# Adding the two state products of every second scan step on GpSimd instead of in TensorE's accumulation

## Chip, core and metric

One core of a Trainium2 chip runs the whole program in one launch. The metric is the device time in microseconds (us), as the median of several runs. One execution was also recorded by the hardware profiler; spans, durations and waits below come from that execution.

## What is computed

Four blocks follow one another on a batch of 8 images of 64 channels and 64 x 64 pixels: an attention and depthwise convolution block, two window-attention blocks with MLPs, a dynamic 3 x 3 filter block, and a state-space block. The change lies in the scan of the last one. For each image and each of four directions k, with 128 channels d and 16 states n, it runs along all 4096 positions:

```python
def step(h, inp):
    u_t, dt_t, B_t, C_t = inp
    h = h * jnp.exp(dt_t[..., None] * A) + dt_t[..., None] * B_t[:, :, None, :] * u_t[..., None]
    return (h, jnp.einsum('bkcn,bkn->bkc', h, C_t))
```

The last line is what matters here: the output y of a position is the sum over the 16 states of h times C.

## The kernel before

**The scan.** Channels lie on the 128 partitions, positions in the free dimension. A unit is one image, one direction and one chunk of TD = 512 positions; it has eight steps of two states each. There are 8 images x 4 directions x 8 chunks x 8 steps = 2048 steps. A step i goes through these places:

- `fetch` (L1670) loads two rows of B or of C from DRAM onto all partitions, a 128x1024 tile, through SP's DMA queue. B and C have three buffers each.
- `products` (L1677) multiplies B by dt x u on GpSimd into a tile `vd` of 128x1024 (L1680). `vd` has six buffers; a buffer is free again when TensorE has read it.
- `step` (L1682): for each of the two states ScalarE computes exp(dt A) into PSUM (L1700), VectorE runs the scan over the 512 positions (L1703), ScalarE copies the last column into `carry` for the next chunk (L1711). Then h is multiplied by C into the same `vd`.
- `sums` (L1719) adds both halves of `vd` into one PSUM tile `yd`, with a matmul by the identity each (L1730). Sixteen such matmuls make one unit's y. At the unit's end VectorE adds `yd` to the image's sum Y (L1739 to L1744).

**Two forms of the product with C.** The variable `rp` (L1689) is 0 in even steps of the images 0 to 5. There GpSimd multiplies both states in one 128x1024 instruction (L1714). In odd steps, and in all steps of the images 6 and 7, GpSimd multiplies the first state (L1716, 128x512) and VectorE the second (L1717).

**What lies beside the scan.** `tile_kernel` runs `front(0)`, the first three blocks and the scan's inputs for the first two images, by itself. Then `scans(p)` runs the scan of the image pair p and, between its steps, pieces of other work: `back(p-1)`, which is the scan's output projection and the closing convolutions of the pair before, and `front(p+1)`. Each piece is a `yield` with a cost; after each scan step, pieces are emitted until their cost keeps pace with the step (L1639). So a given piece of the other work stands beside a given step. The fourth pair has only `back(2)` beside it, and `back(3)` runs alone at the end.

**What sets the order.** A scheduler takes the instructions in about the order in which they were emitted, works out which are ready, and fixes one order for each engine. Each engine then takes its own queue strictly in that order. One order is written out by hand: `behind` (L1731) puts the first sum matmul of step i-1 behind the product with C of step i in the schedule (`st["w"]`), without a wait.

Of the kernel before, what the change touches and what calls it, by code (L numbers as in the profile page):

```python
# [11 lines left out]
ALU = mybir.AluOpType  # L12
# [11 lines left out]
DI, NST, RNK, KDIR = 128, 16, 4, 4  # L24
# [201 lines left out]
class _Net:  # L226
# [353 lines left out]
    def in_range(self, pool):  # L580

        nc, tc = self.nc, self.tc
        m = self.sums.shape[1] * 64
        m2 = m + 2 * 4 * NH
        n = m2 + B * KDIR * NTD
        sums = self.sums.rearrange("p a b c -> p (a b c)")
        ok = pool.tile([P, n], F32, name="ok", tag="ok")
        top = pool.tile([P, n], F32, name="top", tag="top")
        cnt = self.const.tile([P, 1], F32, name="cnt", tag="cnt")
        bad = self.const.tile([1, 1], mybir.dt.int32, name="bad", tag="bad")  # L590
        nc.vector.tensor_scalar(ok[:, 0:m], sums, 1e-28, None, ALU.is_gt)
        nc.vector.tensor_scalar(top[:, 0:m], sums, 1e28, None, ALU.is_lt)
        nc.vector.tensor_tensor(ok[:, 0:m], ok[:, 0:m], top[:, 0:m], ALU.mult)
        for i, test in enumerate((ALU.is_lt, ALU.is_gt)):
            ws = self.wsum[:, i].rearrange("p b c -> p (b c)")
            d = ok[:, m + 4 * NH * i : m + 4 * NH * i + 4 * NH]
            nc.vector.tensor_scalar(d, ws, (1e28, 1e-28)[i], None, test)
        nc.vector.tensor_scalar(
            ok[:, m2:n], self.esum.rearrange("p a b c -> p (a b c)"), 1e28, None, ALU.is_lt
        )  # L600
        nc.vector.tensor_reduce(cnt, ok, AX.X, ALU.add)
        with tc.tile_pool(name="psr", bufs=1, space=PSUM) as ps:
            pc = ps.tile([1, 1], F32, name="pcnt", tag="pcnt")
            nc.tensor.matmul(pc, lhsT=cnt, rhs=self.ones[:, 0:1], start=True, stop=True)
            nc.vector.tensor_scalar(bad, pc, P * n - 0.5, None, ALU.is_lt)
        return nc.values_load(bad[0:1, 0:1], min_val=0, max_val=1, skip_runtime_bounds_check_because="a comparison gives 0 or 1")
# [541 lines left out]
class _Direct:  # L1148
# [82 lines left out]
    def layer0(self, p):  # L1231
# [11 lines left out]
        with tc.tile_pool(name="w0", bufs=2) as wk:  # L1243
# [38 lines left out]

            sums = net.sums[:, p]
            nc.vector.tensor_reduce(sums, parts, AX.X, ALU.add)
            rec = wk.tile([P, 2, 32], F32, name="rec", tag="rec", bufs=1)
            nc.vector.reciprocal(rec, sums)
# [395 lines left out]
    def step(self, i, st):  # L1682

        nc, w, net = self.nc, self.w, self.net
        wk, ps = self.sw, self.ps
        u = self.units[i // 8]
        k, c, at, CC, v = u["k"], u["c"], u["at"], st["C"], st["v"]

        n0, rp = 2 * (i % 8), i % 2 or u["image"] >= B - 2  # L1689
        rev = k >= 2  # L1690

        def along(t):
            return t[:, ::-1] if rev else t

        h = wk.tile([P, 2 - i % 2, TD], F32, name="hd", tag=f"h{i % 2}", bufs=1)
        hs = []
        for j in range(2):
            n = n0 + j
            da = ps.tile([P, TD], F32, name="dad", tag="da")
            nc.scalar.activation(da, u["du"][:, 0], AF.Exp, scale=net.As[:, k, n : n + 1])  # L1700
            first = 0.0 if at == 0 else self.carries[:, n : n + 1]
            to = da if rp and j else h[:, j]
            nc.vector.tensor_tensor_scan(along(to), along(da), along(v[:, j]), first, ALU.mult, ALU.add)  # L1703
            hs.append(to)
            if at < NTD - 1 and (rp or j):
                ends = h[:, :, 0] if rev else h[:, :, TD - 1]
                cs = self.carries[:, n0 : n0 + 2]
                if rp:
                    ends = to[:, 0:1] if rev else to[:, TD - 1 : TD]
                    cs = self.carries[:, n : n + 1]  # L1710
                nc.scalar.activation(cs, ends, AF.Copy)  # L1711

        if rp == 0:
            st["w"] = nc.gpsimd.tensor_tensor(v, h, CC, ALU.mult)  # L1714
        else:
            st["w"] = nc.gpsimd.tensor_tensor(v[:, 0], h[:, 0], CC[:, 0], ALU.mult)  # L1716
            nc.vector.tensor_tensor(v[:, 1], hs[1], CC[:, 1], ALU.mult)  # L1717

    def sums(self, i, st, after=None):  # L1719

        nc, w, net = self.nc, self.w, self.net
        wk, ps = self.sw, self.ps
        u = self.units[i // 8]
        k, c = u["k"], u["c"]
        if i % 8 == 0:
            u["y"] = ps.tile([P, TD], F32, name="yd", tag="y", bufs=1)
        y = u["y"]
        for j in range(2):
            n = 2 * (i % 8) + j
            m = nc.tensor.matmul(y, lhsT=w["ident"], rhs=st["v"][:, j], start=(n == 0), stop=(n == NST - 1))  # L1730
            if after is not None and j == 0:  # L1731
                net.behind(m, after)
        if i % 8 < 7:
            return

        yd = net.part(self.Y, k, c)
        yp = y.rearrange("p (a b) -> p a b", b=64)
        if u["nth"] == 0:
            nc.vector.scalar_tensor_tensor(yd, self.img(u["x"]), net.dsum, yp, ALU.mult, ALU.add)  # L1739
        elif u["nth"] < 3:  # L1740
            nc.vector.tensor_tensor(yd, yd, yp, ALU.add)  # L1741
        else:
            o = wk.tile([P, TD], F32, name="yo", tag="yo", bufs=1)
            nc.vector.tensor_tensor(self.img(o), yd, yp, ALU.add)  # L1744
            nc.sync.dma_start(u["out"][:, c * TD : (c + 1) * TD], o)
# [134 lines left out]
```

## Time and profile before

The median of three runs is 14083.28 us (14071.26 to 14084.42). The profiled execution took 14074.21 us; its span, from the first to the last instruction, is 14072.3 us, at a mean granted TensorE clock of 0.865.

| stage (what stands beside the scan) | us | steps with L1714 | TensorE busy | VectorE busy | GpSimd busy |
|---|---|---|---|---|---|
| front(0) alone, 0 to 1905 | 1905 | 0 | 1597 | 400 | 2 |
| attention, 1905 to 2983 | 1078 | 76 | 993 | 502 | 630 |
| depthwise convolution, to 3179 | 196 | 20 | 137 | 180 | 162 |
| windows and MLP, to 4159 | 980 | 90 | 865 | 721 | 744 |
| layer 2, to 4551 | 392 | 30 | 364 | 239 | 242 |
| scan sources and back, to 5188 | 637 | 58 | 430 | 476 | 482 |
| back, pooling part, to 5433 | 245 | 16 | 161 | 195 | 131 |
| attention, to 6266 | 833 | 52 | 793 | 307 | 421 |
| depthwise convolution, to 6462 | 196 | 17 | 136 | 166 | 151 |
| windows and MLP, to 7393 | 931 | 76 | 826 | 637 | 617 |
| layer 2, to 7736 | 343 | 20 | 320 | 181 | 174 |
| scan sources and back, to 8569 | 833 | 77 | 547 | 610 | 637 |
| back, pooling part, to 8716 | 147 | 10 | 87 | 140 | 75 |
| attention, to 9647 | 931 | 57 | 881 | 348 | 477 |
| depthwise convolution, to 9843 | 196 | 19 | 135 | 181 | 160 |
| windows and MLP, to 10725 | 882 | 72 | 788 | 599 | 580 |
| layer 2, to 11117 | 392 | 25 | 362 | 215 | 205 |
| scan sources and back, to 11690 | 573 | 56 | 368 | 429 | 454 |
| fourth pair and the end, to 14072 | 2382 | 0 | 1548 | 1907 | 1830 |

The limits of the stages are those of the lines that run in them (attention L1258, windows L1420 and L1492, layer 2 L1541). A busy time is the time in which the engine had at least one instruction under way. Instructions that lie across a limit are counted on both sides, so the third column adds up to 771 where there are 768. One L1714 stands for a pair of steps, an even and an odd one: four state products summed by TensorE. In a profile line, the first number after the bar is the busy time of the group in us, the second the mean duration of one in ns; what follows is the idle time of the engine just before, and what ended it. PEld is TensorE's loading of weights, which lies beside the matmuls.

### The profile page before, as it was taken

How to read it: one execution, taken by the hardware profiler on the slowest of the kernel's cores; microseconds unless marked ns; L12 is line 12 of the kernel's file. 1: busy time of each engine (PE TensorE's matmuls, PEld its weight loads, DVE VectorE, ACT ScalarE, POOL GpSimd, SP SyncE). 2: the span in 40 equal slices, each digit the busy share in tenths (PEclk: the TensorE clock that was granted, in tenths of full speed). 3: DMA queues.
4: the chain of work that ended last, by engine and by line, in shares of the span. 5: the costliest groups of instructions: out<-in, count | busy, mean ns of one | idle time of the engine just before them, and what ended most of it. 6: DMA issues, size and time to landing. Idle time of an engine off the chain costs nothing. (4 is left out here: it accounts for less than half of the span.)

```text
span 14072.3 us, 141532 instructions
## 1 busy us (share of the span) xinstructions
PE 11340.1 (81%) x46358; PEld 4189.8 (30%) x46358; DVE 8432.1 (60%) x9763; ACT 7036.3 (50%) x15453; POOL 8173.2 (58%) x4111
## 2 busy tenths in 40 slices
PE   9888879979889668998889666998988866666665
PEld 2244222224433222223433222222443222222221
DVE  0222254467776875347675767336666677998884
ACT  5533145555553645555562644555554454454442
POOL 0000035677776765456674685456666678879991
PEclk9866679989889889998898788999888878988996
DMA  0000034456555764345553675345554577878882
GB/s 17 1 1 1 5 136 153 161 187 211 195 196 181 241 206 156 127 147 181 175 197 133 225 247 180 128 144 175 170 173 168 181 244 256 276 241 291 294 291 70
DMA packets 705498, 2379.22 MB, mean 169 GB/s; under 512 B 81060, under 2 KB 81188, under 8 KB 703980
## 3 DMA queue, kind: packets, MB, share of 16 engines
q1 hardware_dynamic: 681024, 2315.57, 48.5%
q10 hardware_dynamic: 23724, 54.50, 1.0%
q8 instruction: 367, 6.01, 0.2%
q14 instruction: 383, 3.14, 0.1%
HBM read 2269.08 MB, written 100.66 MB: 168 GB/s over the span
## 5 line engine op out<-in xcount | busy, mean ns | idle before, releaser
L1680 POOL TENSOR_TENSOR vd<-B,du 128x1024 f32<-128x1024 f32 x2048 | 4842.5, 2369 | 3955.8 <-DVE xacc L1217 1888.8
L1730 PE MATMUL yd<-vd,pack 128*128 128x512 f32 x8192 | 4577.0, 686 | 1175.1 <-POOL vd L1714 419.8
L1703 DVE TENSOR_TENSOR_SCAN hd<-dad,carry,vd 128x512 f32<-128x512 f32 x2464 | 3092.6, 1270 | 1081.7 <-ACT dad L1700 681.2
L1700 ACT ACTIVATE dad<-du,As 128x512 f32<-128x512 f32 x4096 | 2711.7, 679 | 985.0 <-DVE hd L1703 728.8
L1730 PEld LDWEIGHTS yd<-vd,pack 128*128 128x128 f32 x8192 | 1592.5, 212 | 3853.7 <-issue 1753.0
L1714 POOL TENSOR_TENSOR vd<-hd,C 128x1024 f32<-128x1024 f32 x768 | 1810.9, 2358 | 1365.4 <-DVE hd L1703 694.1
L1716 POOL TENSOR_TENSOR vd<-hd,C 128x512 f32<-128x512 f32 x1280 | 1634.9, 1278 | 271.7 <-DVE hd L1703 244.6
L1272 ACT ACTIVATE e<-s 128x512 f32<-128x512 f32 x2048 | 1199.2, 591 | 1030.0 <-PE s L1266 1028.1
L1703 DVE TENSOR_TENSOR_SCAN dad<-dad,carry,vd 128x512 f32<-128x512 f32 x1120 | 1426.0, 1273 | 62.7 <-ACT dad L1700 62.5
L1266 PE MATMUL s<-X 64*128 64x512 f32 x4096 | 1350.1, 646 | 114.1 <-ACT e L1272 113.8
L1258 PE MATMUL po<-e,VT 128*64 128x512 f32 x4096 | 1145.1, 629 | 17.0 <-ACT e L1272 17.0
L1711 ACT ACTIVATE carry<-hd 128x1 f32<-128x1 f32 (+1 forms) x1792 | 357.1, 201 | 1172.7 <-DVE hd L1703 1161.9
L1717 DVE TENSOR_TENSOR vd<-dad,C 128x512 f32<-128x512 f32 x1280 | 858.7, 671 | 82.1 <-ACT carry L1711 74.8
L1266 PEld LDWEIGHTS s<-X 64*128 64x128 f32 x4096 | 365.3, 186 | 1065.4 <-issue 820.8
L1420 PEld LDWEIGHTS w_av<-vals,w_e 64*64 64x64 f32 x16384 | 612.7, 159 | 178.0 <-ACT w_e L1410 69.9
L1420 PE MATMUL w_av<-vals,w_e 64*64 64x9 f32 x16384 | 638.5, 216 | 23.6 <-ACT w_e L1410 23.5
L1703 DVE TENSOR_TENSOR_SCAN hd<-dad,vd 128x512 f32<-128x512 f32 x352 | 420.2, 1210 | 203.0 <-ACT dad L1700 92.0
L1741 DVE TENSOR_TENSOR Y<-Y,yd 128x512 f32<-128x512 f32 x128 | 124.6, 973 | 656.0 <-PE yd L1730 655.7
L1410 ACT ACTIVATE w_e<-w_e 128x512 f32<-128x512 f32 x512 | 310.4, 627 | 382.2 <-DVE w_e L1405 254.9
L1655 PE MATMUL pdd<-xs,xdt 128*128 128x512 f32 x512 | 323.4, 718 | 204.3 <-DVE hd L1703 96.7
L1711 ACT ACTIVATE carry<-dad 128x1 f32<-128x1 f32 x1120 | 189.9, 170 | 589.1 <-DVE dad L1703 587.0
L1405 DVE TENSOR_TENSOR w_e<-w_s,bias 128x512 f32<-128x512 f32 x512 | 328.5, 682 | 248.4 <-PE w_s L1393 248.1
(247 smaller groups left out, 11078.1 us busy)
## 6 DMA issues: line engine op xcount, KB each, us to landing
B<-rows SPq DMA_DIRECT2D x2048, 512.0 KB, 5.0
C<-rows SPq DMA_DIRECT2D x2048, 512.0 KB, 4.5
xs<-xt SPq DMA_DIRECT2D x128, 256.0 KB, 2.9
xs<-xc SPq DMA_DIRECT2D x128, 256.0 KB, 3.1
xc<-xcv ACTq DMA_DIRECT2D x64, 256.0 KB, 4.3
zs<-z ACTq DMA_DIRECT2D x64, 256.0 KB, 3.9
xt<-XT ACTq DMA_DIRECT2D x32, 512.0 KB, 7.5
rows<-bc SPq DMA_DIRECT2D x256, 64.0 KB, 1.9
```

The source lines that it names most:

```text
L1258: nc.tensor.matmul(po[half[im]], lhsT=VT[:, t, half[im]], rhs=es[im], start=(t == 0), stop=(t == 31))
L1266: nc.tensor.matmul(ss[im], lhsT=at(half[im], t), rhs=X[half[im], jc * CH : (jc + 1) * CH], start=True, stop=True)
L1272: nc.scalar.activation(e, ss[im], AF.Exp, scale=C**-0.5, accum_out=parts[:, im, t, jc : jc + 1])
L1420: nc.tensor.matmul(self.av[half[im], x % 4 + j, h, :], lhsT=es[h // 4][half[im], j, h % 4, :], rhs=V[half[im], x + j, h, :], start=True, s ...
L1680: self.nc.gpsimd.tensor_tensor(v, st["B"], dx.to_broadcast([P, 2, TD]), ALU.mult)
L1700: nc.scalar.activation(da, u["du"][:, 0], AF.Exp, scale=net.As[:, k, n : n + 1])
L1703: nc.vector.tensor_tensor_scan(along(to), along(da), along(v[:, j]), first, ALU.mult, ALU.add)
L1711: nc.scalar.activation(cs, ends, AF.Copy)
L1714: st["w"] = nc.gpsimd.tensor_tensor(v, h, CC, ALU.mult)
L1716: st["w"] = nc.gpsimd.tensor_tensor(v[:, 0], h[:, 0], CC[:, 0], ALU.mult)
L1717: nc.vector.tensor_tensor(v[:, 1], hs[1], CC[:, 1], ALU.mult)
L1730: m = nc.tensor.matmul(y, lhsT=w["ident"], rhs=st["v"][:, j], start=(n == 0), stop=(n == NST - 1))
```

## The change

In even steps of the images 0 to 5, after the product of both states with C, GpSimd adds the second half of `vd` to the first, in place. `sums` then issues one matmul for such a step in place of two; the flags that open and close the accumulation are worded anew for that. `st["w"]`, behind which the sum of the step before is ordered, is now the add in those steps. Odd steps, and all steps of the images 6 and 7, are as before.

```diff
         if rp == 0:
-            st["w"] = nc.gpsimd.tensor_tensor(v, h, CC, ALU.mult)
+            nc.gpsimd.tensor_tensor(v, h, CC, ALU.mult)
+            st["w"] = nc.gpsimd.tensor_tensor(v[:, 0], v[:, 0], v[:, 1], ALU.add)
+            st["n"] = 1
         else:
...
         y = u["y"]
-        for j in range(2):
-            n = 2 * (i % 8) + j
-            m = nc.tensor.matmul(y, lhsT=w["ident"], rhs=st["v"][:, j], start=(n == 0), stop=(n == NST - 1))
+        n = st.get("n", 2)
+        for j in range(n):
+            m = nc.tensor.matmul(
+                y, lhsT=w["ident"], rhs=st["v"][:, j], start=(i % 8 + j == 0), stop=(i % 8 == 7 and j == n - 1)
+            )
             if after is not None and j == 0:
                 net.behind(m, after)
```

In the changed kernel the product is on L1714, the add on L1715, the odd step's products on L1718 and L1719, and the sum matmul on L1732.

## The prediction, on record before the result

> **What bounds the kernel now.** The changed lines run only where image < 6, from 1905 us (first product) to about 11690 us. I read in this order: the busy time by stage, the costliest groups, the time line of one stretch of each kind, the waits. First the stages of the second image pair (the table ahead has all of them):
>
> ```profile
> core 0: us, PE busy (x) PEld busy (x) DVE busy (x) ACT busy (x) POOL busy (x), PEclk, DMA share, GB/s
> ...
> 5433.00:6266.00 833.00, 793.25 (x2386) 215.30 (x2384) 307.38 (x290) 478.18 (x1376) 420.77 (x205) 0.97 0.39 133
> 6266.00:6462.00 196.00, 136.32 (x372) 52.55 (x369) 165.57 (x194) 88.70 (x182) 150.94 (x72) 0.84 0.58 202
> 6462.00:7393.00 931.00, 826.08 (x6929) 404.76 (x6928) 637.05 (x817) 540.46 (x1028) 616.57 (x300) 0.88 0.53 180
> 7393.00:7736.00 343.00, 320.00 (x626) 116.19 (x625) 180.78 (x211) 97.69 (x197) 174.12 (x84) 0.90 0.40 136
> 7736.00:8569.00 833.00, 547.45 (x926) 183.84 (x924) 610.37 (x656) 449.74 (x841) 636.73 (x308) 0.82 0.68 233
> ```
>
> No engine bounds the whole span. Attention (first row) and layer 2 (fourth) leave TensorE busy 95% and 93%, GpSimd 51%. The sources and back stage (last) has TensorE at 66% and GpSimd at 76%. The windows (third) lie between. So the change takes work from the engine that is last in some stages and gives it to the one that is last in others. The prices, from the page's groups:
>
> ```profile
> L1680 POOL TENSOR_TENSOR vd<-B,du 128x1024 f32<-128x1024 f32 x2048 | 4842.5, 2369 | 3955.8 <-DVE xacc L1217 1888.8
> L1730 PE MATMUL yd<-vd,pack 128*128 128x512 f32 x8192 | 4577.0, 686 | 1175.1 <-POOL vd L1714 419.8
> ...
> L1714 POOL TENSOR_TENSOR vd<-hd,C 128x1024 f32<-128x1024 f32 x768 | 1810.9, 2358 | 1365.4 <-DVE hd L1703 694.1
> L1716 POOL TENSOR_TENSOR vd<-hd,C 128x512 f32<-128x512 f32 x1280 | 1634.9, 1278 | 271.7 <-DVE hd L1703 244.6
> ```
>
> There are 4096 sum matmuls in the code and 8192 records on L1730: one instruction is two records, and 686 ns is not the price of one instruction. The attention stretch gives it:
>
> ```profile
> 5700.91 1.98 PE L1730 MATMUL yd<-vd,pack 128*128 128x512 f32 x4
> ...
> 5702.82 1.13 PE L1266 MATMUL s<-X 64*128 64x512 f32 x4
> ...
> 5721.13 1.12 PE L1655 MATMUL pdd<-xs,xdt 128*128 128x512 f32 x2
> ...
> 5722.19 1.05 PE L1664 MATMUL pbc<-xs,pack 128*32 128x512 f32 x2
> ```
>
> Four records hold the queue from 5700.91 to 5702.82, 1.91 us; two records of the same shape from 5721.13 to 5722.19, 1.06 us. So one sum matmul less is 0.85 us of the queue at full clock. In the other kind of stretch GpSimd has no gap at all:
>
> ```profile
> 8203.21 2.35 POOL L1680 TENSOR_TENSOR vd<-B,du 128x1024 f32<-128x1024 f32 x1
> 8205.51 2.35 POOL L1714 TENSOR_TENSOR vd<-hd,C 128x1024 f32<-128x1024 f32 x1
> 8207.82 2.36 POOL L1680 TENSOR_TENSOR vd<-B,du 128x1024 f32<-128x1024 f32 x1
> 8210.13 1.27 POOL L1716 TENSOR_TENSOR vd<-hd,C 128x512 f32<-128x512 f32 x1
> 8211.36 2.37 POOL L1680 TENSOR_TENSOR vd<-B,du 128x1024 f32<-128x1024 f32 x1
> ```
>
> Two steps, 8.15 us, four instructions end to end: here the add must lengthen the pair.
>
> **What the Trainium skill says.** "GPSIMD Engine Reference", section "Elementwise — side-by-side cycle accounting", gives 4497 ns for an add of 2048 fp32 elements, about twice VectorE. A quarter, 512 elements, is 1124 ns by an estimate from that page; L1716 takes 1278 ns for the multiply of that shape, and I use the trace. The same page, section "Instruction dispatch", says that consecutive Pool instructions are no barrier between its cores, so that a read of what another core has just written needs a wait on the completion semaphore. In the build the add does wait on GpSimd's own semaphore. Its price is not in the trace of before as such: back to back, L1716 to L1680 is 1.23 us from start to start, 0.04 less than its duration, so losing that overlap costs at least 0.05 us. "Advanced Engine Details and Errata", section "GPSIMD Details", says GpSimd shares a read and a write interface with VectorE, in conflict with VectorE instructions that have two SBUF inputs. The trace agrees: L1766, which has two, takes 723 ns at best and 4773 at most. Scans (1270 ns) have one input in PSUM and stay level. L1766 and its like are few, and I put no term for them.
>
> **The change part by part.** Of each pair of steps (even, odd), 768 pairs, one sum matmul goes and one 128x512 add comes.
>
> Removed: 768 x 0.85 = 653 us of TensorE's queue. Added: 768 x 1.27 = 975 us of GpSimd. Neither sum is the time; each counts where its engine is last. The pairs by stage are the L1714 counts in the table.
>
> Attention, 185 pairs: TensorE 94%, GpSimd 54%, going to 1528 + 235 = 1763 of 2685 us, 66%. The add hides, and the sums do not wait: in 5433 to 6266 TensorE's queue waits for L1714 five times, 4.9 us in all. Saved 185 x 0.85 = 157. The instruction order of the two builds places the even sums at the same point among the attention matmuls.
>
> Layer 2, 75 pairs: the same. Saved 75 x 0.85 = 64.
>
> Windows and MLP, 238 pairs, clock 0.88: 0.97 us each at most, 230. But here sums already stand at the head of TensorE's queue waiting for the C product; from the waits of 3179 to 4110 us:
>
> ```profile
> PEld yd L1730 <- POOL vd L1714: 42.9, 28, 3.5
> ```
>
> 28 waits there, 18 in 6462 to 7295, 15 in 9843 to 10627. Behind a waiting sum stand all later window matmuls, and the add comes between product and sum. In the first pair's windows GpSimd goes from 744 to 744 + 90 x 1.27 = 858 of 980 us, 88%: no gain there. For the other 148 pairs I take half, 0.48: 71. What takes the other half is the wait for the add.
>
> Sources and back, 191 pairs: TensorE has slack, so nothing is gained. In slices of 49 us, GpSimd is at 87% or more in those that start at 4551, 4600, 4894 and 4992, and from 8079 to 8324 and 11411 to 11607, together 74 pairs by the product counts: full price, 74 x 1.27 = 94. In the other 117 pairs GpSimd waits for scans and for B now; part of that covers the add. Bounds 0 and 1.27; I take half, 75. Lost 169.
>
> Depthwise convolution, 56 pairs: VectorE 90%, GpSimd 8.4 us of a pair's 10.5, with the add 9.7. It fits, but barely; bounds 0 and 1.27, taken 0.4: 22 lost. Pooling part of the back, 26 pairs: VectorE 86%, GpSimd 53%: nothing.
>
> Moved: the scheduler puts the add right behind its product in 444 cases of 768, behind the odd step's product in 251, behind a B product in 73; then the even sum is later by up to 2.5 us or a later product by 1.3. Stage boundaries stay at the same step in both builds. C is still freed by the product; the B and C loads on SP's queue follow GpSimd's pace and add no term. Nothing before 1905 or after 11690 changes.
>
> Sum: 157 + 64 + 71 - 169 - 22 = 101 us saved. The profiled execution took 14074.2 us (span 14072.3); minus 101 is 13973. The median of the runs is 9 above the profiled one, so 13982.
>
> **The rivals.** GpSimd becomes the bound (slower). Place: sources and back, with the in-order window stage. Price: all 191 pairs pay 1.27 = 243, depthwise half of 71, windows gain nothing: 221 - 243 - 35 = -57, 14140; with the full 71 and 61 window waits longer by 1.27 (77), 170 slower, 14253. It decides once the windows give nothing and sources and back pay more than 0.91 of the full price. For it: the stretch without a gap, and that all GpSimd work stands in one queue, so that an add also delays the B products that the next scans need. Against it: GpSimd's own waits for scans, 45 us from 4551 to 5188 and 78 from 7736 to 8569, which need not grow.
>
> TensorE is last wherever it is at 88% or more. Windows give all 230, sources and back lose half of 169: 157 + 64 + 230 - 85 = 366, 13717. For it: 89% busy in the windows. Against: 69% to 76% GpSimd there, and the 61 waits.
>
> The two cancel: within 28 us of 14083. That needs 0.5 us more per pair in sources and back, well inside its bounds.
>
> That the change does not act is no rival: the build has 3328 sum matmuls in the direct path and 768 adds.
>
> **How the numbers follow.** Main case 0.52 (13982, own range 13900 to 14050), TensorE everywhere 0.12 (13717), cancel 0.13 (14083), GpSimd the bound 0.23 (14140 to 14253). About 0.2% (28 us) is what a measurement of this kernel can tell from no change. Faster 0.52 + 0.12 = 0.64, same 0.13, slower 0.23. The range's low end has two thirds of the window term (153) and 69 lost in sources and back: 157 + 64 + 153 - 69 - 22 = 283, 13800. Its high end has no window term, sources and back in full and depthwise nearly so: 157 + 64 - 243 - 65 = -87, 14170. The far ends of both outer cases are left out.
>
> **What would show it.** Right: attention and layer 2 stages shorter by about 0.85 us a pair (52 pairs: 44 us), GpSimd without gaps in sources and back, those stages longer by about 0.9 us a pair, L1715 at about 1.27 us. Wrong: attention stages that do not shorten (then TensorE was not last), an add far from 1.27 us, or windows longer by waits for the add, which brings the slower rival.

## The result, and the profile after

The changed kernel takes 14319.48 us, median of four runs (14298.49 to 14339.54); the kernel before takes 14077.27 us in the four runs beside it. The ratio is 1.0173, with a 95% interval of 1.0152 to 1.0194: 1.7% slower, 242 us. The forecast was 101 us faster, and the time lies above the stated range. The profiled execution has a span of 14336.0 us (before 14072.3), and the mean granted clock fell from 0.865 to 0.825.

First the groups of the page of the changed kernel that answer to those shown before:

```profile
L1680 POOL TENSOR_TENSOR vd<-B,du 128x1024 f32<-128x1024 f32 x2048 | 4829.6, 2367 | 3397.4 <-DMA B<-rows 2053.3
L1732 PE MATMUL yd<-vd,pack 128*128 128x512 f32 x6656 | 4033.6, 729 | 1494.1 <-POOL vd L1715 719.3
...
L1714 POOL TENSOR_TENSOR vd<-hd,C 128x1024 f32<-128x1024 f32 x768 | 1812.2, 2360 | 1234.9 <-DVE hd L1703 743.1
L1718 POOL TENSOR_TENSOR vd<-hd,C 128x512 f32<-128x512 f32 x1280 | 1633.9, 1278 | 236.8 <-DVE hd L1703 209.0
...
L1715 POOL TENSOR_TENSOR vd<-vd 128x512 f32<-128x512 f32 x768 | 980.5, 1277 | 34.8
```

The instructions are those foreseen: 768 adds of 1277 ns, 980 us of GpSimd; 1536 matmul records fewer. But the records that are left grew from 686 to 729 ns, and TensorE waits for the add for 719 us in all. Next, the busy times by stage of the changed kernel, second image pair, each stage cut at its own first and last instructions (columns as before: length, then busy us of TensorE, weight loads, VectorE, ScalarE, GpSimd, then the clock, the DMA share and GB/s):

```profile
5526.00:6389.00 863.00, 811.85 (x2424) 215.97 (x2422) 332.61 (x314) 507.14 (x1462) 526.63 (x278) 0.96 0.42 142
6389.00:6630.00 241.00, 153.32 (x418) 58.18 (x417) 203.55 (x234) 120.77 (x239) 217.99 (x114) 0.79 0.62 206
6630.00:7516.00 886.00, 747.20 (x6586) 378.94 (x6588) 576.37 (x743) 493.36 (x927) 640.34 (x339) 0.83 0.51 170
7516.00:7886.00 370.00, 332.63 (x658) 119.63 (x657) 202.18 (x243) 110.15 (x223) 210.95 (x112) 0.87 0.41 137
7886.00:8947.00 1061.00, 635.89 (x995) 208.91 (x995) 753.93 (x833) 527.11 (x970) 838.84 (x440) 0.73 0.60 209
```

The limits of the rows shown before were rounded to slices of the page; cut in the same way, attention in the kernel before reads:

```profile
5389.20:6282.40 893.20, 848.09 (x2533) 230.79 (x2532) 333.39 (x315) 509.76 (x1461) 455.11 (x221) 0.97 0.40 136
```

So attention is 30 us shorter. The windows, 854 us before by the same cut, are longer although TensorE has less to do, and the clock fell in every stage. In the stretch of kind "GpSimd without a gap", the time line of GpSimd now reads:

```profile
8398.86 2.34 POOL L1714 TENSOR_TENSOR vd<-hd,C 128x1024 f32<-128x1024 f32 x1
8401.27 1.26 POOL L1715 TENSOR_TENSOR vd<-vd 128x512 f32<-128x512 f32 x1
8402.49 2.34 POOL L1680 TENSOR_TENSOR vd<-B,du 128x1024 f32<-128x1024 f32 x1
8404.79 1.27 POOL L1718 TENSOR_TENSOR vd<-hd,C 128x512 f32<-128x512 f32 x1
8406.01 2.36 POOL L1680 TENSOR_TENSOR vd<-B,du 128x1024 f32<-128x1024 f32 x1
8408.33 2.35 POOL L1714 TENSOR_TENSOR vd<-hd,C 128x1024 f32<-128x1024 f32 x1
```

From product to product it is 9.47 us where it was about 8.15: the pair pays 1.32 us. The add starts 2.41 us after the product in front of it, where a following instruction without that wait starts after 2.31: the wait on GpSimd's own semaphore costs 0.10 us.

To see where the time went, I cut both executions at the same instructions: attention's first and last (L1258), the first window matmul (L1420), the last of the MLP (L1492), of layer 2 (L1541), and of the scan sources (L1596). The last row runs on to the next attention, or to the end. Two experiments that are explained below stand beside them. In us:

| stage, three pairs summed | before | without the add | add, not read | changed kernel |
|---|---|---|---|---|
| attention | 2733 | 2676 | 2682 | 2682 |
| depthwise convolution | 654 | 673 | 718 | 720 |
| windows and MLP | 2653 | 2614 | 2744 | 2790 |
| layer 2 | 1186 | 1118 | 1178 | 1168 |
| sources, back and the end | 4838 | 4851 | 4974 | 4967 |

Each column is one profiled execution. That of the kernel without the add took 33 us more than the median of its runs, that of the changed kernel 18 us more. A stage in which nothing was changed can differ by 10 us between two kernels: the first pair's windows take 946 us before and 935 in the run below that changes only later attention stages. The scan steps do not stay in their stages either: in the second pair VectorE ran 80 scans in the depthwise stage before and 93 without the add, and 95 and 83 in layer 2, so part of what layer 2 gains is work that moved to the depthwise stage.

### The profile page after: what moved, and what is told of

The parts are those of the page before. It is cut to its first block, busy times and chain, and to the rows that moved or that the text cites. A ratio compares the mean times of both kernels' runs of the same rounds, so it can differ in the third digit from the quotient of the medians.

```text
span 14336.0 us, 139216 instructions
## 1 busy us (share of the span) xinstructions
PE 11109.3 (77%) x44822; PEld 4039.0 (28%) x44822; DVE 8429.9 (59%) x9763; ACT 7036.8 (49%) x15459; POOL 9125.6 (64%) x4879
## 5 line engine op out<-in xcount | busy, mean ns | idle before, releaser
L1732 PE MATMUL yd<-vd,pack 128*128 128x512 f32 x6656 | 4033.6, 729 | 1494.1 <-POOL vd L1715 719.3
L1714 POOL TENSOR_TENSOR vd<-hd,C 128x1024 f32<-128x1024 f32 x768 | 1812.2, 2360 | 1234.9 <-DVE hd L1703 743.1
L1732 PEld LDWEIGHTS yd<-vd,pack 128*128 128x128 f32 x6656 | 1331.7, 223 | 3918.2 <-issue 1352.8
L1718 POOL TENSOR_TENSOR vd<-hd,C 128x512 f32<-128x512 f32 x1280 | 1633.9, 1278 | 236.8 <-DVE hd L1703 209.0
L1258 PE MATMUL po<-e,VT 128*64 128x512 f32 x4096 | 1200.8, 639 | 33.2 <-ACT e L1272 33.2
L1715 POOL TENSOR_TENSOR vd<-vd 128x512 f32<-128x512 f32 x768 | 980.5, 1277 | 34.8
L1719 DVE TENSOR_TENSOR vd<-dad,C 128x512 f32<-128x512 f32 x1280 | 860.3, 672 | 62.9 <-ACT carry L1711 51.8
L1420 PEld LDWEIGHTS w_av<-vals,w_e 64*64 64x64 f32 x16384 | 647.3, 167 | 197.4 <-ACT w_e L1410 78.3
L1420 PE MATMUL w_av<-vals,w_e 64*64 64x9 f32 x16384 | 673.6, 220 | 30.3 <-ACT w_e L1410 28.8
L1205 PE MATMUL pv<-n_sq,pack 128*128 128x512 f32 x576 | 374.2, 736 | 155.1 <-ACT n_sq L1203 154.7
```

The source lines that it names most:

```text
L1258: nc.tensor.matmul(po[half[im]], lhsT=VT[:, t, half[im]], rhs=es[im], start=(t == 0), stop=(t == 31))
L1420: nc.tensor.matmul(self.av[half[im], x % 4 + j, h, :], lhsT=es[h // 4][half[im], j, h % 4, :], rhs=V[half[im], x + j, h, :], start=True, s ...
L1715: st["w"] = nc.gpsimd.tensor_tensor(v[:, 0], v[:, 0], v[:, 1], ALU.add)
```

## The experiments

Theories after the result. W: the sum at the head of TensorE's queue waits for the add, and all matmuls behind it stand. G: the 975 us more of GpSimd's queue are paid for, although GpSimd is 58% busy. Beside them a question: what are the 768 removed matmuls worth by themselves? Percentages are the ratio to the kernel before, with intervals; us are those percentages of 14077. Medians of the same kernel before differ by up to 0.13%. The edits are shown against the changed kernel, that of the add alone against the kernel before.

**Removed matmuls alone.**

```diff
-            nc.gpsimd.tensor_tensor(v, h, CC, ALU.mult)
-            st["w"] = nc.gpsimd.tensor_tensor(v[:, 0], v[:, 0], v[:, 1], ALU.add)
+            st["w"] = nc.gpsimd.tensor_tensor(v, h, CC, ALU.mult)
             st["n"] = 1
```

> The changed kernel without the add: even steps still send one sum matmul in place of two, so the second state of even steps is left out of y. It measures what the removed matmuls alone are worth. If a removed matmul is worth its 0.85 us wherever TensorE is at 88% or more (498 pairs), it takes 13,620 to 13,750 us against 14,077 before. If removing them brings little because other waits take their place or the granted clock falls, it takes 13,900 to 14,050.

Measured 13905.57 us, ratio 0.9875 (0.9858 to 0.9891): 176 us, or 0.23 us for a matmul whose price in the queue is 0.85. The second, smaller outcome is right. The clock of the profiled execution is 0.831, against 0.852 with the add alone (below), so most of its fall comes with the removed matmuls.

**The add, but nobody waits for its result.**

```diff
-            st["w"] = nc.gpsimd.tensor_tensor(v[:, 0], v[:, 0], v[:, 1], ALU.add)
+            st["w"] = nc.gpsimd.tensor_tensor(v[:, 1], v[:, 0], v[:, 1], ALU.add)
```

> The changed kernel, but the add writes the second half of vd, and the one matmul of an even step reads the first: the second state is left out of y, the add costs GpSimd the same, and no matmul has to wait for its result. Theory W (the wait): the sum at the head of TensorE's queue waits for the add and everything behind it stands; then this is within 100 us of the kernel without the add. Theory G (GpSimd's time): the 975 us more of GpSimd's queue are the loss; then this stays near the changed kernel, above 14,230 us.

Measured 14307.14 us, ratio 1.0165 (1.0148 to 1.0182). TensorE's weight loads wait 70 us for the add in this run, against 1096 us in the changed kernel, and the time is nearly that of the changed kernel. W falls as the main cause; G holds. The difference to the kernel without the add is 2.9%, 408 us, 0.53 us for each add. By the table the windows are 46 us longer where the result is read, and no other stage is; the medians of the two kernels differ by 12 us only, which is inside the intervals.

**Every sum one step later.**

```diff
-                if i:
-                    self.sums(i - 1, steps[i - 1], steps[i]["w"])
+                if i > 1:
+                    self.sums(i - 2, steps[i - 2], steps[i]["w"])
```

The last two sums follow after the loop.

> The changed kernel with every sum emitted one step later: sums of step i-2 behind step i, in place of i-1; all of the computation is kept. Theory W: the add is done before the sum stands at the head of TensorE's queue; at least 120 us faster than the changed kernel, 14,050 to 14,200 us. Theory G: no change from the changed kernel within 40 us, or slower, since a vd buffer is held one step longer.

Measured 14468.50 us, ratio 1.0287 (1.0267 to 1.0306): slower than the changed kernel. TensorE's matmuls do wait less for the add, 312 us against 719. But a `vd` buffer is held a step longer. Scans waiting for a B product, in the attention stage of the second pair, first here, then in the changed kernel:

```profile
DVE hd L1704 <- POOL vd L1681: 153.0, 31, 10.8
```

```profile
DVE hd L1703 <- POOL vd L1680: 33.2, 14, 6.1
```

The wait is moved, not removed: part of it now lies in front of the scans. That the extra time comes from there is argued, not shown.

**The add on VectorE.**

```diff
-            st["w"] = nc.gpsimd.tensor_tensor(v[:, 0], v[:, 0], v[:, 1], ALU.add)
+            st["w"] = nc.vector.tensor_tensor(v[:, 0], v[:, 0], v[:, 1], ALU.add)
```

> The changed kernel with the add on VectorE in place of GpSimd, in the same place; all of the computation is kept. An add there takes about 0.67 us (from the products on VectorE). Theory G: GpSimd's time is as before, so most of the loss goes: 13,950 to 14,080 us. Theory W: the sum now waits in VectorE's queue behind scans; 14,150 us or more.

Measured 14889.40 us, ratio 1.0579 (1.056 to 1.0599). The size falls under W, but not for W's reason. The add's own row in this run (least, median and greatest duration in ns):

```profile
L1715 DVE TENSOR_TENSOR vd<-vd x768: 664/1736/2894, 1945.9 to 12486.1; 128x512 f32<-128x512 f32 x192
```

An add that takes 664 ns at best takes 1736 in the median, and VectorE stands idle 675 us before it until GpSimd's product is done, with the scans behind it. The 148 adds that ran with no GpSimd instruction beside them took 675 to 694 ns; the 347 that lay wholly beside GpSimd's work took 1739 in the median. So this run does not tell W from G; it shows that the other engine is no way out.

**The add alone, both matmuls kept.**

```diff
-            st["w"] = nc.gpsimd.tensor_tensor(v, h, CC, ALU.mult)
+            nc.gpsimd.tensor_tensor(v, h, CC, ALU.mult)
+            st["w"] = nc.gpsimd.tensor_tensor(CC[:, 0], v[:, 0], v[:, 1], ALU.add)
```

> The kernel before, with both sum matmuls kept, plus an add of the same shape and place on GpSimd whose result lands in the first half of the used C tile and is read by nobody. The add alone: with one matmul less it cost 402 us (14,307 against 13,906). If that price holds whatever TensorE does, this takes about 14,475 us. If TensorE's work, longer here by 653 us, covers part of the add, it takes 14,230 to 14,380 us, and the removed matmuls are worth that much less beside an add.

Measured 14527.05 us, ratio 1.0322 (1.0303 to 1.034): 453 us, 0.59 us an add. With TensorE's full work in place the add is not hidden better; it costs as much or a little more. In the whole time the two parts nearly add up: -1.25% and +3.22% make 1.97%, the two together gave 1.65%. By stages they do not: in attention the add alone costs 130 us (2733 to 2863) and the removed matmuls give 57, and yet the two together are 51 us shorter than before. The next run shows what stands between.

**Half an add.**

```diff
-            st["w"] = nc.gpsimd.tensor_tensor(v[:, 0], v[:, 0], v[:, 1], ALU.add)
+            st["w"] = nc.gpsimd.tensor_tensor(v[:, 1, 0:256], v[:, 0, 0:256], v[:, 1, 0:256], ALU.add)
```

> As the changed kernel with the add that nobody reads, but over 256 positions in place of 512, about 0.7 us in place of 1.27; the second state of even steps is left out of y. If GpSimd's time is the price, in proportion: 13,906 + 402 x 0.7/1.27 = 14,130 us, within 50. If the price lies in having one more instruction with a wait on its own engine, it stays above 14,230 us.

Measured 14123.53 us, ratio 1.0031 (1.0015 to 1.0048): 1.56% above the kernel without the add. The half add takes 725 ns, 0.57 of the whole one; 0.57 of 2.9% is 1.65%. The price goes with GpSimd's time, and not with one more instruction or its wait.

Here a rival has to be set aside. The scheduler works out each engine's order anew for every edit, so two kernels may differ in more than the edit. The traces show the order on each engine. In the half add, the add that is not read and the changed kernel, TensorE, ScalarE, VectorE and GpSimd start their instructions in the same order from end to end. So from half an add to a whole one nothing but its duration changes: 0.55 us more for each costs 1.34%, 189 us, 0.25 us an add. Every stage pays: attention 31 us, depthwise 15, windows 44, layer 2 16, the rest 71. The kernels without the add, with the add alone and before have other orders; a difference between two of these is that of the edit and of the new order together.

**The add behind the next B product.** The add is emitted in the next turn of the loop, after `products(i + 2)`.

```diff
+            if i > 0 and "n" in steps[i - 1]:
+                t = steps[i - 1]["v"]
+                self.nc.gpsimd.tensor_tensor(t[:, 0], t[:, 0], t[:, 1], ALU.add)
             if i >= 0:
                 self.step(i, steps[i])
...
-            nc.gpsimd.tensor_tensor(v, h, CC, ALU.mult)
-            st["w"] = nc.gpsimd.tensor_tensor(v[:, 0], v[:, 0], v[:, 1], ALU.add)
+            st["w"] = nc.gpsimd.tensor_tensor(v, h, CC, ALU.mult)
```

> The changed kernel with the add emitted after the next B product in place of before it; all of the computation is kept. If the loss comes from B products, and so scans, that stand behind the add: 14,150 to 14,250 us. If any place in the queue costs the same, within 50 us of the changed kernel's 14,319.

Measured 14407.13 us, ratio 1.0234 (1.0218 to 1.0251), about 90 us slower than the changed kernel. Letting the next product pass first gains nothing; TensorE's wait for the add grows from 719 to 913 us. From the second pair on this kernel has the order of the kernel without the add, except for some 20 places on ScalarE, VectorE and GpSimd. Against that one, the attention stages of the second and third pair are 25 and 30 us longer, for 56 adds each: at the same order the add does not hide there.

**Which adds of a unit cost.** Here and in the next two, the whole computation is kept, and the steps without the change go as before.

```diff
-            nc.gpsimd.tensor_tensor(v, h, CC, ALU.mult)
-            st["w"] = nc.gpsimd.tensor_tensor(v[:, 0], v[:, 0], v[:, 1], ALU.add)
-            st["n"] = 1
+            st["w"] = nc.gpsimd.tensor_tensor(v, h, CC, ALU.mult)
+            if i % 8 < 4:
+                st["w"] = nc.gpsimd.tensor_tensor(v[:, 0], v[:, 0], v[:, 1], ALU.add)
+                st["n"] = 1
```

(its counterpart has `i % 8 >= 4`)

> The change only in steps 0 and 2 of each unit's eight, 384 adds and 384 matmuls fewer; steps 4 and 6 as before, all of the computation kept. If an add costs the same wherever it stands: half of the changed kernel's 242 us, 14,200 us within 30, and equal to its counterpart in steps 4 and 6. If the start of a unit, where GpSimd has a run of B products to do, sets the price, this is the slower of the two by 80 us or more.

> The change only in steps 4 and 6 of each unit's eight, 384 adds and 384 matmuls fewer; steps 0 and 2 as before, all of the computation kept. If an add costs the same wherever it stands: 14,200 us within 30, equal to its counterpart. If the end of a unit, where the next unit's B products and inputs have to be ready, sets the price, this is the slower of the two by 80 us or more.

Measured 14132.83 us, ratio 1.0052 (1.0032 to 1.0071), and 14261.37 us, ratio 1.0137 (1.0116 to 1.0159). Together 1.89%, about the 1.73% of the whole. The second half costs more than twice as much net as the first. The next unit's run of B products stands behind those adds in GpSimd's queue, but nothing shows that this is the reason, and the order of the queues is a better candidate: of the 105 us between the two profiled executions, 86 lie in attention. In attention of the second pair ScalarE runs three of the scan's exponentials in a row in the kernel before (first line), where the changed kernel runs one, then one of attention's (second line):

```profile
5396.12 1.89 ACT L1700 ACTIVATE dad<-du,As 128x512 f32<-128x512 f32 x3
```

```profile
5533.37 0.67 ACT L1700 ACTIVATE dad<-du,As 128x512 f32<-128x512 f32 x1
```

In the attention stages of the second and third pair the second-half kernel has the order of the kernel before on all four engines, and takes 907 and 905 us against 893: at that order half of the change makes them 14 and 12 us longer. The first-half kernel has the changed kernel's order on TensorE, ScalarE and VectorE, and takes 861, about as the changed kernel with all its adds (863). That is 32 us less than before, more than the 28 sums gone are worth by the queue (28 x 0.85 = 24). So what the changed kernel gains in these stages comes at least in part with the new order. The first pair shows no such gain: its attention is 27 us longer in the first-half kernel.

**The change in chosen stages.** The condition for the change is the pair number q = i // 2 inside `scans(p)`.

```diff
+            q, p = i // 2, u["image"] // 2
+            if (178 <= q < 208) if p == 0 else (25 <= q < 81 or 170 <= q < 194):
...
```

> The change only in the steps that stand beside attention of the second and third pair (pairs of steps 25 to 81) and beside layer 2 (178 to 208 of the first pair, 170 to 194 of the others); elsewhere as before, all of the computation kept. If attention and layer 2 keep the 30 and 15 us per stage that the changed kernel's stages showed, 13,970 to 14,010 us. If the scan steps that fall behind there are paid for in the depthwise stage that follows, 14,040 to 14,100 us, no change.

Measured 14013.35 us, ratio 0.9951 (0.9936 to 0.9967). This beats both kernels. Attention gives 28 us in each of the two pairs, layer 2 gives 12 and 15, and the depthwise stages pay only 5 and 4. Layer 2 of the first pair is 10 us longer, and the windows of the second and third pair 13 and 4.

**In attention alone.**

```diff
+            if p > 0 and 25 <= q < 81:
...
```

> The change only in the steps beside attention of the second and third pair (pairs of steps 25 to 81), as before elsewhere, all of the computation kept. In the selected version those two stages gave 28 us each, layer 2 gave 12 and 15 and lost 10 in the first pair, and the windows lost 13 and 4. If the windows' loss comes from attention's scan steps that fall behind: 14,030 to 14,060 us. If it belongs to layer 2: 14,010 to 14,030 us.

Measured 14021.44 us, ratio 0.9967 (0.9959 to 0.9976). Attention gives 28 us twice and the depthwise stages pay nothing. That is most of what the chosen stages gave; the difference to them is inside the intervals. The windows after it are 6 and 10 us longer than before, but the first pair's windows, where nothing was changed, are 10 us shorter, so this does not decide between the two branches of the expectation. ScalarE's order among attention's instructions is another than before here too, so the gain is that of the edit with its order.

**A quarter of the removed matmul put back.**

```diff
+        if n == 1:
+            nc.tensor.matmul(y[:, 0:128], lhsT=w["ident"], rhs=st["v"][:, 1, 0:128], start=False, stop=False)
```

> The kernel without the add (13,906 us), with a matmul over 128 of the 512 positions in place of the one that even steps no longer send; the rest of the second state of even steps is left out of y. About a quarter of the removed work comes back, some 160 us of TensorE's queue. If the removed work counts for its time alone, a quarter of the 168 us is lost again: 13,930 to 13,970 us, clock 0.84. If the removed matmuls are worth little because fewer instructions let the clock fall, the clock comes back to 0.86 and the time stays at or under 13,906 us.

Measured 13973.47 us, ratio 0.9927 (0.9903 to 0.9951), clock 0.839. In the time line the even step's sum with the small matmul behind it holds the queue for 1.28 us, where the sum alone, in the kernel without the add, holds it for 1.06. So the small one adds 0.22 us, 26% of 0.85. What is lost again is 0.52% of 1.25%, 42%, but the intervals allow 18% to 65%. That agrees with a worth in proportion to the work, at the low rate, and does not pin it down. The clock rises with the work too, and did not go back to 0.86 with the number of instructions.

## Why the prediction was wrong

**The sum in short.** The forecast had 292 us gained in attention, layer 2 and windows, and 191 lost. The runs give 176 us for all removed matmuls, 408 lost to the adds even when nobody reads their result, and 11 for the reading, which is inside the noise. Two steps failed: the price of a removed matmul, and "The add hides".

**Durations and counts were right.** The add takes 1277 ns for the 1270 used, the wait on GpSimd's own semaphore costs 0.10 us where at least 0.05 was said, and a pair in the stretch without a gap pays 1.32 us.

**"Sources and back, 191 pairs: ... Lost 169"** held in kind: the last row of the table lost 129 us.

**"Saved 185 x 0.85 = 157" in attention failed in size.** The stages are 51 us shorter: 30 in the second and the third pair, and 9 longer in the first. Those 30 come at least in part with the new order, as the first-half and second-half runs show; the prediction had looked at the place of the even sums on TensorE, which is indeed the same, and not at ScalarE's queue. "Layer 2: saved 64" gave 18. Without any add, attention, windows and layer 2 together gain 57 + 39 + 68 = 164 us, where their matmuls are worth up to 157 + 230 + 64 by the queue. So the price of 0.85 us was wrong even before the add comes in, though this kernel's order is a new one as well. Look at the four front stages of the second pair, attention to layer 2, first before, then without the add (168 pairs, columns as above):

```profile
5389.00:7738.00 2349.00, 2117.85 (x10413) 800.93 (x10413) 1313.09 (x1532) 1229.74 (x2845) 1386.84 (x672) 0.91 0.47 158
```

```profile
5345.00:7645.00 2300.00, 2034.47 (x10078) 767.27 (x10074) 1308.59 (x1533) 1231.11 (x2848) 1385.66 (x672) 0.88 0.47 162
```

Busy time multiplied by the clock is work at full clock: 2118 x 0.91 = 1927, and 2034 x 0.88 = 1790. That is 137 us less, as 168 x 0.85 = 143 says. But only 83 us of it appear as less busy time, since TensorE runs at a lower clock, and idle time grows from 231 to 266. What remains is 49 us. The Trainium skill, in "TensorE: Matmul & The Clock Gate", section "What's actually happening", says that the throttled clock is the default and activity releases it. The runs agree: 0.865 before, 0.839 with a part of the matmuls gone, 0.831 with all of them gone. In sources and back of the first pair the clock falls from 0.82 to 0.73 with no change in the stage's length (852 and 850 us). The whole run says the same: TensorE's busy time by the clock is 11340 x 0.865 = 9809 us before and 11021 x 0.831 = 9158 without the add, 651 us less, as 653 were foreseen, while busy time itself fell by 319. That the lower clock costs time is an account from the records; no run here holds the clock and removes the work.

**"The add hides" failed.** It was argued from busy shares: GpSimd at 54% to 69% has room. It has room on the average of a stage only. The add alone costs 0.59 us each with TensorE's whole work beside it, goes with its duration, and costs 130 us in the windows even when nobody reads its result (about 222 pairs, 0.59 each), where the forecast had a gain of 71. In layer 2, "the same" as attention in the prediction, it costs 60. In attention the table shows 6 us only, but these two kernels differ in order; at the same order the pairs of runs above show 31 us from half to whole add, and 25 and 30 in one stage each. What is late next is seen in the waits of the four front stages of the second pair. First without the add, then with the add that is not read:

```profile
ACT dad L1700 <- DVE hd L1703: 127.0, 114, 4.9
...
DVE hd L1703 <- POOL vd L1714: 41.1, 42, 4.4
```

```profile
ACT dad L1700 <- DVE hd L1703: 170.4, 128, 5.6
...
DVE hd L1703 <- POOL vd L1714: 85.2, 43, 5.0
```

The scan of the next even step writes `hd`, of which there is one buffer, and can start only when the product with C has read it; that product comes later when GpSimd's queue is longer. ScalarE's next exponential waits for the scan. Behind that exponential, in ScalarE's one queue, stand those of attention and of the windows, for which TensorE waits. So GpSimd's time comes back through three queues to the engine that looked like the bound. From half to whole add, at the same order, the same two waits grow, from 159.3 to 170.4 and from 68.6 to 85.2 us. But so does a shorter way: TensorE's weight loads wait longer for GpSimd's later products with C, 55.1 to 67.3 us in even steps and 39.1 to 49.1 in odd ones. And of the 31 us that these four stages grow there, 24 are busy time of TensorE with the same 10078 records (2036 to 2060 us), as its clock goes from 0.88 to 0.87, and only 7 are idle time. How much of the price each way carries is not shown; that the price is GpSimd's time is.

**"What takes the other half is the wait for the add"** named a true wait of the wrong weight. In the windows of the first pair, 3207 to 4221 us, the line shown before (29 waits, 46 us by the same cut, 3182 to 4128) has become:

```profile
PEld yd L1732 <- POOL vd L1715: 108.9, 46, 6.8
```

It is worth at most 46 us of the windows' loss of 137, less by the medians; the add's time is worth 130, and the removed matmuls gave 39 back. Depthwise convolution, forecast to lose 22, lost 66: 19 of it appears with the removed matmuls alone, where more scan steps fall into that stage than before, and 45 with the add. "Stage boundaries stay at the same step in both builds" thus holds for the order in which instructions are emitted, and not for that in which they run.

**The slower rival had the cause and not the place.** "GpSimd becomes the bound" was given 0.23 and at worst 14253. Its price, in full in sources and back, was too high there (129 of 243), and it left attention and layer 2 with their whole gain, 221, of which 69 came.

## What to carry to other kernels

A busy share near 95% does not price the work that is taken away: here the removed matmuls gave 0.23 us each for 0.85 us of queue, and the clock fell. Price a removal by a run without that work. An average share of 60% does not make room either, where several engines pass one step around through queues in fixed order: price an addition by runs that change its duration. An edit also makes the scheduler deal the queues anew, so compare orders before a difference is put down to the edit; the three kernels of the same order are what carries the argument here. And a trade between two engines can be worth making in one place only: in the attention stages of two pairs the same edit, with the order that came with it, gains 0.33%, and everywhere it loses 1.7%.

## What had not been expected of the hardware

A VectorE add with two inputs in SBUF took 675 to 694 ns with GpSimd idle and 1739 in the median wholly beside its work, up to 2894 in the run, while GpSimd's own instructions grew by some 2% at most (B product 2369 to 2419 ns, product of one state 1278 to 1305). Identical matmuls in the same order took 24 us more busy time in four stages when another engine's instruction grew by 0.55 us a step pair, with the clock at 0.87 in place of 0.88. The mean granted clock fell with TensorE's work, from 0.865 to 0.831 for 768 of 4096 sum matmuls less.
